# A Mamba scan on one core: program order on the compute engines, softplus sums on GpSimd, diagonals of B through DRAM

## The chip, the core and the metric

The kernel runs on one core of a Trainium2 chip. The core has five engines that run side by side, each through its own queue of instructions: TensorE (PE, matrix products into PSUM; PEld in a profile is its weight load), VectorE (DVE), ScalarE (ACT), GpSimd (POOL[...]) and SyncE (SP), which here issues the DMA transfers. An engine takes its own queue in order; between engines, semaphores make one wait for another. The metric is the device time of one execution in microseconds (us); a run is repeated and the median taken.

## What is computed

Four layers in a row on 8 images of 256 channels and 32 x 32 points, all in fp32: a stack of four Mamba blocks with a channel gate and a batch norm, then three attention layers. Only the Mamba part is touched. For one block, with tokens `xs` (8, 1024, 256):

```python
xn = (xs - mu) * rsqrt(var + 1e-05) * lw + lb
xin, z = split(xn @ iw.T, 2)                    # 512 channels each
xin = silu(causal_conv4(xin) + cb)              # depthwise, 4 taps
proj = xin @ xw.T                               # 16 + 16 + 16 columns
dt = softplus(proj[..., :16] @ dw.T + db)       # (8, 1024, 512)
Bm, Cm = proj[..., 16:32], proj[..., 32:]
A = -exp(alog)                                  # (512, 16)
def step(h, t):                                 # h: (8, 512, 16)
    h = h * exp(dt_t[..., None] * A) + (dt_t * x_t)[..., None] * b_t[:, None, :]
    return h, einsum('bdn,bn->bd', h, c_t)
y = scan(step) + xin * dp
xs = xs + (y * silu(z)) @ ow.T
```

## The kernel before

The Mamba phase works in units: one layer, one image, one half of 512 tokens; 4 x 8 x 2 = 64 units. A unit has 16 steps: 2 pairs of channel tiles (`q`) by 8 groups (`g`) of 2 of the 16 states. In each step TensorE makes the forced term `bx` = B times dt times x by a product with diagonal matrices `dg`; ScalarE makes the decays `da` = exp(dt A); VectorE runs four scans over 512 tokens; GpSimd multiplies the states by C (`ct`, loaded by DMA into all partitions); TensorE sums over the states into `y`, two steps later (LAG = 2).

```python
def forced(s, q, g, i):
    bx = ps_b.tile([P, T, NG], F32, ...)                 # PSUM, 2 buffers
    for k in range(NB):
        for h in range(2):
            for r in range(2):
                nc.tensor.matmul(bx[...], lhsT=s["dtxT"][q][...], rhs=s["dg"][g][h * H:(h + 1) * H, k, :, :], start=True, stop=True)
    return bx

def state(i, k, bx):                                     # cut: the carry of the first half
    for j in range(NG):
        init = 0.0 if c == 0 else st["h"][:, q, g, k, j:j + 1]
        nc.vector.tensor_tensor_scan(hs[i][:, k, j, :], das[i][2 * k + j], bx[:, :, j], init, ALU.mult, ALU.add)

def product(i):
    if s["c"] < NCH - 1:
        nc.scalar.copy(s["st"]["h"][:, q, g, :, :], h[:, :, :, T - 1])      # hc
    nc.gpsimd.tensor_tensor(h, h, cts.pop(i).unsqueeze(1).to_broadcast([P, 2, NG, T]), ALU.mult)
```

The rest of a unit is written as three generators, of which a few pieces are run behind each step: `inward` (norm, input projection, convolution) two units ahead, `onward` (projections to dt, B and C, softplus, the transposed `dtxT`) one unit ahead, `outward` (output projection, residual sum) for the unit before. Each `yield` ends a piece; `AT` says behind which steps the pieces stand.

```python
LAG, AHEAD = 2, 2
AT = ((inward, 2, (0, 1, 2, 3, 5, 6, 8, 9, 11, 12, 13, 14)), (onward, 1, (1, 3, 5, 7, 8, 9, 10, 11, 12)),
      (outward, -1, (3, 4, 6, 7, 9, 10, 11, 12, 13)))
DIAGONALS = (4, 5, 6, 10, 11, 12, 13, 14)
for i in range(len(steps) + LAG):
    n, at = divmod(i, per_unit)
    if i < len(steps):
        ahead(i + AHEAD)                     # load of ct and the 4 decays of step i + 2; 8 buffers da
        bxs = [forced(*steps[i], k) for k in range(2)]
        for k in range(2):
            state(i, k, bxs[k])
        product(i)
    if i >= LAG:
        for j in range(NG):
            summed(s, q, g, j, hs[i - LAG])  # y; dd first where g == 0
        if g == NGR - 1:
            gate(s, q)
    ...                                      # the pieces of AT, then
    if at in DIAGONALS and n + 1 < len(units):
        diagonal(units[n + 1])
```

The pieces that the change and the prediction touch. All PSUM tiles with the tag "mm" share two buffers:

```python
# inward, second piece
rstd = sq[:, 0, :]
nc.scalar.activation(rstd, pvar, AF.Ln, bias=eps)
nc.scalar.activation(rstd, rstd, AF.Exp, scale=-0.5)
nc.vector.tensor_tensor(xn, xn, rstd.unsqueeze(1).to_broadcast([P, CT, T]), ALU.mult)         # L136
# inward, last piece: the gate activation, then the table of exp and ln again
for q in range(DT // 2):
    nc.scalar.activation(s["xin"][q], s["xin"][q], AF.Silu)
nc.scalar.activation(sz, sz, AF.Silu)
exp_ln_table()

# onward
for q in range(DT // 2):
    for r in range(2):
        pd = ps_m.tile([P, T], F32, ..., tag="mm")
        nc.tensor.matmul(pd, lhsT=w["dt"][...], rhs=tokens(proj[...]), start=True, stop=True)
        nc.scalar.activation(e[:, r, :], pd, AF.Abs, bias=col(V_DB + i))
        nc.scalar.activation(dt[:, r, :], pd, AF.Relu, bias=col(V_DB + i))
    nc.scalar.activation(e, e, AF.Exp, scale=-1.0)
    yield
    nc.scalar.activation(one, e, AF.Identity, bias=1.0)
    nc.scalar.activation(ln, one, AF.Ln)
    nc.vector.scalar_tensor_tensor(e, one, 1.0, e, ALU.subtract, ALU.subtract)                # L233
    nc.vector.tensor_tensor(dt, dt, e, ALU.subtract)                                          # L234
    nc.vector.tensor_tensor(dt, dt, ln, ALU.add)                                              # L235
    yield
for q in range(DT // 2):
    for i in range(2):
        nc.gpsimd.tensor_tensor(tokens(dtx[:, i, :]), halves(s["dt"][q][:, i, :]), halves(xin[q][:, i, :]), ALU.mult)
    yield
    for i in range(2):
        pt = ps_m.tile([P, NB, P], F32, ..., tag="mm")
        for k in range(NB):
            nc.tensor.transpose(pt[:, k, :], dtx[:, i, k * P:(k + 1) * P], ident)
        nc.scalar.copy(dtxT[:, i, :, :], pt)
    yield

def diagonal(s):                             # 11 buffers
    nc.gpsimd.tensor_tensor(dg, twin.unsqueeze(1).unsqueeze(3).to_broadcast([P, NB, H, NG]),
                            bt[:, :, NG * g:NG * (g + 1)].unsqueeze(2).to_broadcast([P, NB, H, NG]), ALU.mult)

# outward
for m in range(CT):
    po = ps_m.tile([P, T], F32, ..., tag="mm")
    for i in range(DT):
        nc.tensor.matmul(po, lhsT=w["out"][...], rhs=s["sz"][:, i, :], start=(i == 0), stop=(i == DT - 1))
        if i == 1:
            yield                            # po stays open over a step
    nc.vector.tensor_tensor(x[:, m, :], po, x[:, m, :], ALU.add)                              # xo
```

The instructions are written to a scheduler that keeps their dependences and picks, engine by engine, the order in which they go into the queues. It may pull an instruction ahead of an earlier one that it takes to be waiting. Only the table loads of ScalarE are pinned to their place (`tc.keep_in_program_order`).

Of the kernel before, what the change touches and what calls it, by code (L numbers as in the profile page):

```python
# [19 lines left out]
P = 128  # L20
B, C, HW = 8, 256, 1024
CT = C // P
T = 512
# [13 lines left out]
G_SEB2, G_BNW, G_BNB, G_BQ1, G_BK1, G_BO1, G_BQ2, G_BK2, G_BQ3, G_BK3, G_BO3, G_N = range(0, 24, 2)  # L37


def mamba_phase(tc, ctx, a, spill, ident, gvec, stats):  # L40
    nc = tc.nc
    cst = ctx.enter_context(tc.tile_pool(name="m_cst", bufs=1))
    wp = ctx.enter_context(tc.tile_pool(name="m_w", bufs=1))
    wk1 = ctx.enter_context(tc.tile_pool(name="m_wk1", bufs=1))
# [3 lines left out]
    dgp = ctx.enter_context(tc.tile_pool(name="m_dg", bufs=NGR + 3))  # L48
    dap = ctx.enter_context(tc.tile_pool(name="m_da", bufs=8))
    drp = ctx.enter_context(tc.tile_pool(name="m_dr", bufs=3, space=DRAM))  # L50
    ps_b = ctx.enter_context(tc.tile_pool(name="m_psb", bufs=2, space=PSUM))
    ps_y = ctx.enter_context(tc.tile_pool(name="m_psy", bufs=1, space=PSUM))
    ps_m = ctx.enter_context(tc.tile_pool(name="m_psm", bufs=2, space=PSUM))
# [6 lines left out]
    twin = cst.tile([P, H], F32, name="twin")  # L60
    for r in range(2):
        nc.vector.tensor_copy(twin[r * H:(r + 1) * H, :], ident[r * H:(r + 1) * H, r * H:(r + 1) * H])
    se1 = cst.tile([P, CT, 64], F32, name="se1")
    nc.sync.dma_start(se1, a["se_w1"])
    se2 = cst.tile([64, C], F32, name="se2")
# [39 lines left out]
        nc.sync.dma_start(w["out"], a["m_out"][l])  # L105

    def exp_ln_table():
        tc.keep_in_program_order(nc.scalar.preload_act_table_set("natural_log_exp_and_others"))

    def tokens(t):  # L110

# [5 lines left out]
    def inward(s):  # L117

        l, u, b, c, st = s["l"], s["name"], s["b"], s["c"], s["st"]
        w = s["w"] = layers[l]  # L120
        x = load_x(s, "x")
        pmu = ps_m.tile([P, T], F32, name=f"pmu{u}", tag="mm")
        for k in range(CT):
            nc.tensor.matmul(pmu, lhsT=mean_w, rhs=x[:, k, :], start=(k == 0), stop=(k == CT - 1))
        xn = wk1.tile([P, CT, T], F32, name=f"xn{u}", tag="xn")
        nc.vector.tensor_tensor(xn, x, pmu.unsqueeze(1).to_broadcast([P, CT, T]), ALU.subtract)
        sq = wk1.tile([P, CT, T], F32, name=f"sq{u}", tag="sq")
        nc.scalar.activation(sq, xn, AF.Square)
        yield
        pvar = ps_m.tile([P, T], F32, name=f"pvar{u}", tag="mm")  # L130
        for k in range(CT):
            nc.tensor.matmul(pvar, lhsT=mean_w, rhs=sq[:, k, :], start=(k == 0), stop=(k == CT - 1))
        rstd = sq[:, 0, :]
        nc.scalar.activation(rstd, pvar, AF.Ln, bias=eps)
        nc.scalar.activation(rstd, rstd, AF.Exp, scale=-0.5)
        nc.vector.tensor_tensor(xn, xn, rstd.unsqueeze(1).to_broadcast([P, CT, T]), ALU.mult)  # L136
        yield

        def in_proj(e):
            ps = ps_m.tile([P, T], F32, name=f"pin{u}_{e}", tag="mm")  # L140
            for k in range(CT):
                nc.tensor.matmul(ps, lhsT=w["in"][:, k, e * P:(e + 1) * P], rhs=xn[:, k, :],  # L142
                                 start=(k == 0), stop=(k == CT - 1))
            return ps


        if c == 0:
            st["tail"] = [wk2.tile([P, 2, K - 1], F32, name=f"tail{u}_{q}", tag=f"tail{q}") for q in range(DT // 2)]
        s["xin"] = []
        for q in range(DT // 2):  # L150
            xr = wk1.tile([P, 2, K - 1 + T], F32, name=f"xr{u}_{q}", tag="xr")
            if c == 0:
                nc.gpsimd.memset(xr[:, :, 0:K - 1], 0.0)
            else:
                nc.gpsimd.tensor_copy(xr[:, :, 0:K - 1], st["tail"][q])
            for e in range(2):
                j = 2 * q + e
                ps = in_proj(j)
                nc.scalar.activation(xr[:, e, K - 1:], ps, AF.Identity, bias=w["ib"][:, j:j + 1])
                yield  # L160
            pcs = [ps_m.tile([P, T], F32, name=f"pc{u}_{q}_{r}", tag="mm") for r in range(2)]
            for k in range(K):
                for r in range(2):
                    for e in range(2):
                        j = 2 * q + e
                        nc.tensor.matmul(pcs[r][e * H:(e + 1) * H, :], lhsT=w["cd"][r * H:(r + 1) * H, j * K + k, :],  # L166
                                         rhs=xr[r * H:(r + 1) * H, e, k:k + T], start=(k == 0), stop=(k == K - 1))
            xin = wk5.tile([P, 2, T], F32, name=f"xin{u}_{q}", tag="xin")
            for r in range(2):
                nc.scalar.activation(xin[:, r, :], pcs[r], AF.Identity, bias=w["vec"][:, V_CB + 2 * q + r:V_CB + 2 * q + r + 1])  # L170
            s["xin"].append(xin)
            if c == 0:
                nc.gpsimd.tensor_copy(st["tail"][q], xr[:, :, T:T + K - 1])
            yield

        sz = s["sz"] = wk3.tile([P, DT, T], F32, name=f"sz{u}", tag="sz")
        for e in range(DT):
            ps = in_proj(DT + e)
            nc.scalar.activation(sz[:, e, :], ps, AF.Identity, bias=w["ib"][:, DT + e:DT + e + 1])
            if e < DT - 1:  # L180
# [5 lines that stand above are left out]
        if s["last"] and l + 1 < NL:  # L186
            more_weights(l + 1)
        yield

    def onward(s):  # L190
# [19 lines left out]
            nc.tensor.transpose(pb[:, k, :], proj[X_B:X_B + DS, k * P:(k + 1) * P], ident[X_B:X_B + DS, X_B:X_B + DS])  # L210
        bt = s["bt"] = wk2.tile([P, NB, DS], F32, name=f"bt{u}", tag="bt")
        nc.scalar.copy(bt, pb)
        s["dt"], s["dtxT"], s["dg"] = [], [], []

        for q in range(DT // 2):
            dt = wk3.tile([P, 2, T], F32, name=f"dt{u}_{q}", tag="dt")
            s["dt"].append(dt)
            e = wk1.tile([P, 2, T], F32, name=f"e{u}_{q}", tag="e")
            for r in range(2):
                i = 2 * q + r  # L220
                pd = ps_m.tile([P, T], F32, name=f"pd{u}_{i}", tag="mm")
                nc.tensor.matmul(pd, lhsT=w["dt"][r * H:r * H + DTR, i * P:(i + 1) * P], rhs=tokens(proj[r * H:r * H + DTR, :]),
                                 start=True, stop=True)
# [4 lines that stand above are left out]
            one = wk1.tile([P, 2, T], F32, name=f"one{u}_{q}", tag="dtx")  # L228
            nc.scalar.activation(one, e, AF.Identity, bias=1.0)
            ln = wk1.tile([P, 2, T], F32, name=f"ln{u}_{q}", tag="sq")  # L230
            nc.scalar.activation(ln, one, AF.Ln)  # L231

            nc.vector.scalar_tensor_tensor(e, one, 1.0, e, ALU.subtract, ALU.subtract)  # L233
            nc.vector.tensor_tensor(dt, dt, e, ALU.subtract)  # L234
            nc.vector.tensor_tensor(dt, dt, ln, ALU.add)  # L235
            yield

        for q in range(DT // 2):
# [10 lines left out]
                nc.scalar.copy(dtxT[:, i, :, :], pt)  # L249
            yield  # L250

    def diagonal(s):

        g, bt = len(s["dg"]), s["bt"]
        dg = dgp.tile([P, NB, H, NG], F32, name=f"dg{s['name']}_{g}", tag="dg")
        nc.gpsimd.tensor_tensor(dg, twin.unsqueeze(1).unsqueeze(3).to_broadcast([P, NB, H, NG]),  # L256
                                bt[:, :, NG * g:NG * (g + 1)].unsqueeze(2).to_broadcast([P, NB, H, NG]), ALU.mult)
        s["dg"].append(dg)

    def load_x(s, what):  # L260
# [6 lines left out]
    def outward(s):  # L267
# [36 lines left out]
        exp_ln_table()  # L304
        yield
        for h in range(NCH):
            y = x if h == c else wk1.tile([P, CT, T], F32, name=f"sx{b}_{h}", tag="dtx")
            if h != c:
                nc.sync.dma_start(y, spill[b][h])
            r = wk1.tile([P, CT, T], F32, name=f"res{b}_{h}", tag="e")  # L310
            nc.sync.dma_start(r, a["x"][b].rearrange("(k p) t -> p k t", p=P)[:, :, h * T:(h + 1) * T])
            for m in range(CT):
                nc.vector.scalar_tensor_tensor(y[:, m, :], y[:, m, :], g2[:, m:m + 1], r[:, m, :], ALU.mult, ALU.add)
                nc.vector.bn_stats(stats[:, m, (b * NCH + h) * 6:(b * NCH + h + 1) * 6], y[:, m, :])
            nc.sync.dma_start(spill[b][h], y)
            yield
# [41 lines left out]
    for l in range(NL):  # L358
        for b in range(B):
            st = {}  # L360
            for c in range(NCH):
                units.append({"l": l, "b": b, "c": c, "st": st, "name": f"{l}_{b}_{c}", "last": (b, c) == (B - 1, NCH - 1)})
    steps = [(s, q, g) for s in units for q in range(DT // 2) for g in range(NGR)]
    per_unit = len(steps) // len(units)
    das, cts, hs = {}, {}, {}
# [666 lines left out]
```

## Time and profile before

| | |
|---|---|
| time, median of 3 runs | 10693.12 us (10679.93 to 10694.59) |
| span of the profiled execution | 10677.8 us |
| last scan of the Mamba phase starts at | 8003.1 us |
| TensorE clock granted, mean | 0.961 |
| DMA | 704.91 MB, mean 66 GB/s |

The profile gives, by engine, the busy time and its share of the span; then the span in 40 equal slices, where each digit is the busy share in tenths; then groups of instructions: line of the source, engine, operation, output and inputs by name, shape and count, and behind the bar the busy time and the mean ns of one, and behind the second bar the idle time of the engine just before them with what ended it. The waits list says which engine waited at which line for which line, in total. The timeline lists instructions by start and length. The share of a busy engine is no proof that it is the bound in every stretch: a wait counts only where it is on the path.

### The profile page before, as it was taken

Reading aid. Unit: us, or ns where it says so; the run is one execution under the profiler, and the core shown is the slowest. Engines: PE = TensorE matmul, PEld = TensorE weight load, DVE = VectorE, ACT = ScalarE, POOL = GpSimd, SP = SyncE. Lnnn points to the kernel's source line nnn. Section 1 sums busy time; section 2 is a strip of 40 time slices with the busy share of each in tenths; the row PEclk is TensorE's granted clock in tenths of the full one; section 3 lists DMA queues with packets and bytes.
Section 4 is the critical chain, followed back from the end, with each engine's and each line's share of the span. In section 5 each row is a group of like instructions: output and inputs, shape, how many; then the busy total and the mean of one; then the engine's idle time right before and its main releaser. Section 6 shows DMA issues by size and latency. Waiting matters only on the chain. (4 is left out here: it accounts for less than half of the span.)

```text
span 10677.8 us, 237971 instructions
## 1 busy us (share of the span) xinstructions
PE 9676.4 (91%) x104946; PEld 4868.8 (46%) x104946; DVE 7570.7 (71%) x6419; ACT 6108.2 (57%) x8477; POOL 6709.4 (63%) x2563
## 2 busy tenths in 40 slices
PE   7999998999999989999998988888888999999998
PEld 3444444444444444444444444444443433444433
DVE  4878877777878877877887777777785455544554
ACT  5666666666666766666666666666652233333333
POOL 5777776677777767777776766666671344344346
PEclk9999999999999999999999999999999999999999
DMA  1222222222222222222222222222221000000000
GB/s 64 81 86 86 89 81 81 81 86 84 88 83 82 87 82 86 87 83 84 84 85 83 89 86 86 86 88 88 89 100 40 5 9 9 7 6 1 5 5 9
DMA packets 212557, 704.91 MB, mean 66 GB/s; under 512 B 32640, under 2 KB 33728, under 8 KB 210880
## 3 DMA queue, kind: packets, MB, share of 16 engines
q1 hardware_dynamic: 211520, 689.61, 19.4%
q8 instruction: 830, 13.60, 0.5%
q14 instruction: 207, 1.70, 0.1%
HBM read 637.09 MB, written 52.43 MB: 65 GB/s over the span
## 5 line engine op out<-in xcount | busy, mean ns | idle before, releaser
L392 POOL TENSOR_TENSOR h<-h,ct 128x2048 f32<-128x2048 f32 x1024 | 4683.9, 4581 | 2007.1 <-ACT hc L391 921.9
L335 ACT ACTIVATE da<-dt,A 128x512 f32<-128x512 f32 x4096 | 2847.4, 718 | 2298.7 <-DVE h L385 2283.8
L385 DVE TENSOR_TENSOR_SCAN h<-da,hc,bx 128x512 f32<-128x512 f32 x2048 | 2456.9, 1258 | 692.7 <-PE bx L325 579.9
L385 DVE TENSOR_TENSOR_SCAN h<-da,bx 128x512 f32<-128x512 f32 x2048 | 2332.0, 1198 | 722.9 <-PE bx L325 658.9
L325 PE MATMUL bx<-dg,dtxT 64*64 64x128 f32 x65536 | 2316.7, 281 | 306.1 <-DVE h L385 293.9
L325 PEld LDWEIGHTS bx<-dg,dtxT 64*64 64x64 f32 x65536 | 1950.1, 137 | 1131.0 <-issue 933.4
L349 PE MATMUL y<-h,twin 64*64 64x512 f32 x16384 | 2048.5, 599 | 72.2 <-POOL h L392 72.2
L571 ACT ACTIVATE fp<-fs 128x1024 f32<-128x1024 f32 x768 | 765.4, 1022 | 1435.7 <-PE fs L566 1408.0
L142 PE MATMUL pin<-xn,win 128*128 128x512 f32 x2048 | 1015.9, 619 | 9.8 <-DVE xn L136 5.8
L349 PEld LDWEIGHTS y<-h,twin 64*64 64x64 f32 x16384 | 718.0, 135 | 668.9 <-issue 511.4
L166 PE MATMUL pc<-xr,cd 64*64 64x512 f32 x4096 | 654.1, 695 | 207.8 <-DVE xo L278 207.8
L566 PE MATMUL fs<-fq,fk 32*128 32x512 f32 (+1 forms) x3072 | 723.4, 649 | 56.2 <-ACT fp L652 39.3
L588 DVE TENSOR_TENSOR fz<-fz,fp 128x1024 f32<-128x1024 f32 x384 | 531.3, 1384 | 331.0 <-ACT fp L571 327.0
L588 POOL TENSOR_TENSOR fz<-fz,fp 128x1024 f32<-128x1024 f32 x192 | 477.6, 2487 | 416.2 <-ACT fp L571 412.4
L142 PEld LDWEIGHTS pin<-xn,win 128*128 128x128 f32 x2048 | 349.0, 190 | 676.0 <-issue 405.6
L274 PE MATMUL po<-sz,wo 128*128 128x512 f32 x1024 | 561.7, 676 | 52.3 <-ACT dt L225 52.3
L582 PE MATMUL fo<-fp,fv 128*32 128x512 f32 (+1 forms) x3072 | 597.2, 615 | 0.0
L241 POOL TENSOR_TENSOR dtx<-dt,xin 128x512 f32<-128x512 f32 x256 | 432.8, 1716 | 224.8 <-ACT ln L231 222.2
L256 POOL TENSOR_TENSOR dg<-twin,bt 128x512 f32<-128x512 f32 x512 | 539.0, 1064 | 50.8 <-PE bx L325 37.9
L166 PEld LDWEIGHTS pc<-xr,cd 64*64 64x64 f32 x4096 | 230.4, 154 | 597.2 <-issue 274.5
L235 DVE TENSOR_TENSOR dt<-dt,ln 128x1024 f32<-128x1024 f32 x128 | 470.4, 3675 | 14.4 <-ACT da L335 0.9
L566 PEld LDWEIGHTS fs<-fq,fk 32*128 32x128 f32 (+1 forms) x3072 | 196.1, 185 | 469.4 <-issue 270.2
(391 smaller groups left out, 9160.8 us busy)
## 6 DMA issues: line engine op xcount, KB each, us to landing
ct<-cdr SPq DMA_DIRECT2D x1024, 512.0 KB, 3.7
spill<-xo SPq DMA_DIRECT2D x72, 512.0 KB, 5.3
x<-spill SPq DMA_DIRECT2D x48, 512.0 KB, 4.9
xo<-spill SPq DMA_DIRECT2D x48, 512.0 KB, 3.5
x<-in_x SPq DMA_DIRECT2D x16, 512.0 KB, 5.0
xo<-in_x SPq DMA_DIRECT2D x16, 512.0 KB, 3.7
res<-in_x SPq DMA_DIRECT2D x16, 512.0 KB, 4.2
fx<-spill SPq DMA_DIRECT2D x16, 512.0 KB, 6.4
```

Of the source, the lines that this page charges most:

```text
L142: nc.tensor.matmul(ps, lhsT=w["in"][:, k, e * P:(e + 1) * P], rhs=xn[:, k, :], start=(k == 0), stop=(k == CT - 1))
L166: nc.tensor.matmul(pcs[r][e * H:(e + 1) * H, :], lhsT=w["cd"][r * H:(r + 1) * H, j * K + k, :], rhs=xr[r * H:(r + 1) * H, e, k:k + T], sta ...
L274: nc.tensor.matmul(po, lhsT=w["out"][:, i, m * P:(m + 1) * P], rhs=s["sz"][:, i, :], start=(i == 0), stop=(i == DT - 1))
L325: nc.tensor.matmul(bx[r * H:(r + 1) * H, t:t + H, :], lhsT=s["dtxT"][q][h * H:(h + 1) * H, i, k, r * H:(r + 1) * H], rhs=s["dg"][g][h * H: ...
L335: nc.scalar.activation(da, s["dt"][q][:, i, :], AF.Exp, scale=s["w"]["A"][:, nn:nn + 1])
L349: nc.tensor.matmul(s["y"][r][i * H:(i + 1) * H, :], lhsT=twin[r * H:(r + 1) * H, :], rhs=h[r * H:(r + 1) * H, i, j, :], start=False, stop= ...
L385: nc.vector.tensor_tensor_scan(hs[i][:, k, j, :], das[i][2 * k + j], bx[:, :, j], init, ALU.mult, ALU.add)
L392: nc.gpsimd.tensor_tensor(h, h, cts.pop(i).unsqueeze(1).to_broadcast([P, 2, NG, T]), ALU.mult)
L566: nc.tensor.matmul(scs[h // 2][:, h % 2, :], lhsT=k[r:r + D, m, kt * P:(kt + 1) * P], rhs=q[r:r + D, m, half * T:(half + 1) * T], start=Tr ...
L571: nc.scalar.activation(p, scs[j], AF.Exp, scale=scale)
L582: nc.tensor.matmul(acc["o"][r:r + D, :], lhsT=v[:, kt, m * P + r:m * P + r + D], rhs=ps[h // 2][:, h % 2, :], start=(kt == 0), stop=(kt == ...
L588: add(acc["z"][j], acc["z"][j] if kt > 1 else probs[i - 1][j], ps[j], ALU.add)
```

## The change

Four things, all in the Mamba phase:

- every instruction of TensorE, VectorE, ScalarE and GpSimd is pinned behind the one before it in the source, so that these four queues hold the order of the program. SyncE, and so the DMA issues, stays free;
- the three sums of softplus leave VectorE for GpSimd, with one more pass on ScalarE (1 - one), and the factor of the norm stays in PSUM, so that the product with it reads one operand from SBUF and one from PSUM;
- the diagonals of B are no longer made on GpSimd. Two buffers in DRAM are filled with zeros once; each unit writes its 16 x 512 values of B to their places on the diagonals, in 8 transfers of 512 pieces of 8 bytes, and each diagonal is then loaded whole (256 KB);
- a spare tile at the end of the last layer takes its buffer from another pool.

The aim is that no VectorE instruction of the steady part reads two operands from SBUF while GpSimd works, and that GpSimd has room for the sums.

```diff
--- before.py
+++ after.py
@@ -37,8 +37,28 @@
 G_SEB2, G_BNW, G_BNB, G_BQ1, G_BK1, G_BO1, G_BQ2, G_BK2, G_BQ3, G_BK3, G_BO3, G_N = range(0, 24, 2)
 
 
+class InOrder:
+
+
+    def __init__(self, tc, engine):
+        self.tc, self.engine = tc, engine
+
+    def __getattr__(self, name):
+        def call(*args, **kwargs):
+            return self.tc.keep_in_program_order(getattr(self.engine, name)(*args, **kwargs))
+
+        return call
+
+
+class Engines:
+    def __init__(self, tc):
+        nc = tc.nc
+        self.tensor, self.vector, self.scalar, self.gpsimd = (InOrder(tc, e) for e in (nc.tensor, nc.vector, nc.scalar, nc.gpsimd))
+        self.sync = nc.sync
+
+
 def mamba_phase(tc, ctx, a, spill, ident, gvec, stats):
-    nc = tc.nc
+    nc = Engines(tc)
     cst = ctx.enter_context(tc.tile_pool(name="m_cst", bufs=1))
     wp = ctx.enter_context(tc.tile_pool(name="m_w", bufs=1))
     wk1 = ctx.enter_context(tc.tile_pool(name="m_wk1", bufs=1))
@@ -48,6 +68,7 @@
     dgp = ctx.enter_context(tc.tile_pool(name="m_dg", bufs=NGR + 3))
     dap = ctx.enter_context(tc.tile_pool(name="m_da", bufs=8))
     drp = ctx.enter_context(tc.tile_pool(name="m_dr", bufs=3, space=DRAM))
+    dr1 = ctx.enter_context(tc.tile_pool(name="m_dr1", bufs=1, space=DRAM))
     ps_b = ctx.enter_context(tc.tile_pool(name="m_psb", bufs=2, space=PSUM))
     ps_y = ctx.enter_context(tc.tile_pool(name="m_psy", bufs=1, space=PSUM))
     ps_m = ctx.enter_context(tc.tile_pool(name="m_psm", bufs=2, space=PSUM))
@@ -60,6 +81,13 @@
     twin = cst.tile([P, H], F32, name="twin")
     for r in range(2):
         nc.vector.tensor_copy(twin[r * H:(r + 1) * H, :], ident[r * H:(r + 1) * H, r * H:(r + 1) * H])
+    HALF = H * NB * H * NG
+    diagonals = [dr1.tile([(NGR + 1) * 2 * HALF], F32, name=f"diagonals{k}") for k in range(2)]
+    zero = cst.tile([P, 2 * HALF // P], F32, name="zero")
+    nc.gpsimd.memset(zero, 0.0)
+    for d in diagonals:
+        for g in range(NGR + 1):
+            nc.sync.dma_start(d[g * 2 * HALF:(g + 1) * 2 * HALF].rearrange("(p r) -> p r", p=P), zero)
     se1 = cst.tile([P, CT, 64], F32, name="se1")
     nc.sync.dma_start(se1, a["se_w1"])
     se2 = cst.tile([64, C], F32, name="se2")
@@ -105,7 +133,7 @@
         nc.sync.dma_start(w["out"], a["m_out"][l])
 
     def exp_ln_table():
-        tc.keep_in_program_order(nc.scalar.preload_act_table_set("natural_log_exp_and_others"))
+        nc.scalar.preload_act_table_set("natural_log_exp_and_others")
 
     def tokens(t):
 
@@ -130,10 +158,9 @@
         pvar = ps_m.tile([P, T], F32, name=f"pvar{u}", tag="mm")
         for k in range(CT):
             nc.tensor.matmul(pvar, lhsT=mean_w, rhs=sq[:, k, :], start=(k == 0), stop=(k == CT - 1))
-        rstd = sq[:, 0, :]
-        nc.scalar.activation(rstd, pvar, AF.Ln, bias=eps)
-        nc.scalar.activation(rstd, rstd, AF.Exp, scale=-0.5)
-        nc.vector.tensor_tensor(xn, xn, rstd.unsqueeze(1).to_broadcast([P, CT, T]), ALU.mult)
+        nc.scalar.activation(pvar, pvar, AF.Ln, bias=eps)
+        nc.scalar.activation(pvar, pvar, AF.Exp, scale=-0.5)
+        nc.vector.tensor_tensor(xn, xn, pvar.unsqueeze(1).to_broadcast([P, CT, T]), ALU.mult)
         yield
 
         def in_proj(e):
@@ -210,6 +237,7 @@
             nc.tensor.transpose(pb[:, k, :], proj[X_B:X_B + DS, k * P:(k + 1) * P], ident[X_B:X_B + DS, X_B:X_B + DS])
         bt = s["bt"] = wk2.tile([P, NB, DS], F32, name=f"bt{u}", tag="bt")
         nc.scalar.copy(bt, pb)
+        scatter(s)
         s["dt"], s["dtxT"], s["dg"] = [], [], []
 
         for q in range(DT // 2):
@@ -230,9 +258,10 @@
             ln = wk1.tile([P, 2, T], F32, name=f"ln{u}_{q}", tag="sq")
             nc.scalar.activation(ln, one, AF.Ln)
 
-            nc.vector.scalar_tensor_tensor(e, one, 1.0, e, ALU.subtract, ALU.subtract)
-            nc.vector.tensor_tensor(dt, dt, e, ALU.subtract)
-            nc.vector.tensor_tensor(dt, dt, ln, ALU.add)
+            nc.scalar.activation(one, one, AF.Identity, scale=-1.0, bias=1.0)
+            for t in (one, ln):
+                nc.gpsimd.tensor_tensor(e, e, t, ALU.add)
+            nc.gpsimd.tensor_tensor(dt, dt, e, ALU.add)
             yield
 
         for q in range(DT // 2):
@@ -249,12 +278,21 @@
                 nc.scalar.copy(dtxT[:, i, :, :], pt)
             yield
 
+    def scatter(s):
+
+        d = s["dgd"] = diagonals[s["n"] % len(diagonals)]
+        for h in range(2):
+            for k in range(NB):
+                at = h * HALF + k * H * NG
+                to = d[at:at + NGR * 2 * HALF].rearrange("(g r) -> g r", g=NGR)[:, :H * (NB * H * NG + NG)]
+                to = to.rearrange("g (p r) -> p g r", p=H)[:, :, :NG]
+                nc.sync.dma_start(to, s["bt"][h * H:(h + 1) * H, k, :].rearrange("p (g j) -> p g j", j=NG))
+
     def diagonal(s):
 
-        g, bt = len(s["dg"]), s["bt"]
+        g = len(s["dg"])
         dg = dgp.tile([P, NB, H, NG], F32, name=f"dg{s['name']}_{g}", tag="dg")
-        nc.gpsimd.tensor_tensor(dg, twin.unsqueeze(1).unsqueeze(3).to_broadcast([P, NB, H, NG]),
-                                bt[:, :, NG * g:NG * (g + 1)].unsqueeze(2).to_broadcast([P, NB, H, NG]), ALU.mult)
+        nc.sync.dma_start(dg, s["dgd"][g * 2 * HALF:(g + 1) * 2 * HALF].rearrange("(p b t j) -> p b t j", p=P, b=NB, t=H))
         s["dg"].append(dg)
 
     def load_x(s, what):
@@ -304,7 +342,7 @@
         exp_ln_table()
         yield
         for h in range(NCH):
-            y = x if h == c else wk1.tile([P, CT, T], F32, name=f"sx{b}_{h}", tag="dtx")
+            y = x if h == c else wk2.tile([P, CT, T], F32, name=f"sx{b}_{h}", tag="x")
             if h != c:
                 nc.sync.dma_start(y, spill[b][h])
             r = wk1.tile([P, CT, T], F32, name=f"res{b}_{h}", tag="e")
@@ -359,7 +397,7 @@
         for b in range(B):
             st = {}
             for c in range(NCH):
-                units.append({"l": l, "b": b, "c": c, "st": st, "name": f"{l}_{b}_{c}", "last": (b, c) == (B - 1, NCH - 1)})
+                units.append({"l": l, "b": b, "c": c, "st": st, "n": len(units), "name": f"{l}_{b}_{c}", "last": (b, c) == (B - 1, NCH - 1)})
     steps = [(s, q, g) for s in units for q in range(DT // 2) for g in range(NGR)]
     per_unit = len(steps) // len(units)
     das, cts, hs = {}, {}, {}
```

## The prediction

> **What bounds the kernel now.** I read the page first: busy time by engine, and the 40 slices of the span.
>
> ```profile
> PE 9676.4 (91%) x104946; PEld 4868.8 (46%) x104946; DVE 7570.7 (71%) x6419; ACT 6108.2 (57%) x8477; POOL 6709.4 (63%) x2563
> PE   7999998999999989999998988888888999999998
> DVE  4878877777878877877887777777785455544554
> POOL 5777776677777767777776766666671344344346
> ```
>
> The first 30 slices (about 8030 us) are the Mamba phase, which alone is changed; the attention behind it (about 2650 us) is not, and I carry it over. PE is the fullest engine, at 9 tenths, so what can be won are PE's gaps. They come from the list of waits of 4000 to 5000 us, narrowed to PE (columns: waiter, what it waited for, us in total, times, longest):
>
> ```profile
> PE pc L166 <- DVE xo L278: 27.3, 8, 3.4
> PE bx L325 <- DVE h L385: 25.5, 34, 3.1
> PE pd L222 <- ACT dt L225: 10.4, 8, 1.4
> PE y L349 <- POOL h L392: 7.7, 13, 1.3
> PE pt L248 <- ACT sz L179: 7.6, 9, 1.1
> ```
>
> The first two rows are VectorE being late. Why it is late stands in the groups by line of the same stretch:
>
> ```profile
> L392 POOL TENSOR_TENSOR h<-h,ct 128x2048 f32<-128x2048 f32 x134 | 612.5, 4579 | 231.9 <-ACT hc L391 81.9 <-DVE h L385 64.9 <-PE bx L325 48.5
> L235 DVE TENSOR_TENSOR dt<-dt,ln 128x1024 f32<-128x1024 f32 x16 | 59.5, 3721 | 2.0 <-ACT da L335 0.5
> L233 DVE SCALAR_TENSOR_TENSOR e<-one,e 128x1024 f32<-128x1024 f32 x16 | 19.5, 1216 | 0.0
> L136 DVE TENSOR_TENSOR xn<-xn,sq 128x1024 f32<-128x1024 f32 x8 | 36.5, 4564 | 8.5 <-ACT sq L135 8.5
> ```
>
> L235 and L233 have one size, yet take 3721 and 1216 ns; L136 takes 4564, the length of one GpSimd product (4579). They stand behind that product.
>
> Last the timeline. First, PE where nothing holds it (start, length):
>
> ```profile
> 4141.93 1.90 PE L349 MATMUL y<-h,twin 64*64 64x512 f32 x16
> 4143.75 1.98 PE L142 MATMUL pin<-xn,win 128*128 128x512 f32 x4
> 4145.67 1.98 PE L325 MATMUL bx<-dg,dtxT 64*64 64x128 f32 x64
> 4147.46 1.90 PE L349 MATMUL y<-h,twin 64*64 64x512 f32 x16
> ```
>
> From start to start: y 1.82, pin 1.92, bx 1.79 us. So 3.6 us of PE per step, plus side work. Second, one unit (16 steps), from gate to gate:
>
> ```profile
> 4042.41 1.26 DVE L355 TENSOR_TENSOR sz<-y,sz 128x512 f32<-128x512 f32 x2
> 4162.28 1.26 DVE L355 TENSOR_TENSOR sz<-y,sz 128x512 f32<-128x512 f32 x2
> ```
>
> That is 119.9 us. The side work by the same timeline: pmu, pvar, 8 pin and 4 po halves at 1.92 each, pp 3.5, two pc of 3.75, pt 2.2, pd 2.3, dd 1.7, pb 0.35, together 44.2; with 16 x 3.6 it makes 101.8 us. So PE loses 18 us per unit, 64 units in all.
>
> [...] the trace has 1217 ns at L126, whose second operand is in PSUM. [...] the trace has 4579, and for 1024 elements a median of 2400 (L588), which I use. [...] No transfer of 8 B pieces is in this trace, so their price stays open.
>
> **The change, part by part.**
> 1. Softplus sums and rstd. VectorE loses L233 to L235, (158 + 174 + 470)/64 = 12.5 us per unit, and L136 falls from 4.43 to about 1.22: 15.8 us of its roughly 98. GpSimd gets 6 sums of 2.4 = 14.4 us and loses 8 diagonals, 539/64 = 8.4. ScalarE gets two passes of 1.06 us.
> 2. Diagonals. Per unit 8 scatters of 512 pieces of 8 B, and 8 loads of 256 KB, 2 MB beside the 8 MB of ct. They are made at steps 3 to 14 of the unit before, 11 buffers for 8, so a latency of some us costs nothing. What could cost is the one SyncE queue: ct stands behind the scatter. 4096 pieces over 16 engines are 256 each; at 157 ns (the average packet: 19.4% of 16 x 10678 us over 211520) 40 us, at a third of that 13. The next ct has about 25 us of slack, because GpSimd is then in its sums.
> 3. Program order. Table loads fall from 66 in 1000 us (7.9 per unit) to 2: 7.6 us of ScalarE, which is not the bound. In exchange nothing is pulled ahead any more. I walked one unit by hand: each engine takes its instructions in the order of the source, each starts when its operands and buffer are there. The scans of a step end 5.8 us after its first bx starts (1.27, then 4 x 1.14); the next decays end 0.8 later, since they reuse the scanned buffers; side work of ScalarE comes after them.
>  - Step 3: pin, pb, pd0, pd1, po share two PSUM buffers. pd0 waits for the eviction of pin, behind the decays, and po for Relu of pd0: +3.0 us.
>  - Step 7: one buffer is held by the open po. pd1 waits for Abs and Relu of pd0, which wait for scans and decays (5.8 + 0.8 + 0.2, then 1.3); then pd1 1.05 and po: +4.5 us. Before, po was pulled ahead of pd1 here.
>  - Step 10: pt needs dtx. From the start of step 8: scans 5.8, hc 1.0, product 4.55, sums 7.2, product of step 9 4.55, dtx 1.3 = 24.4. PE gets there after 5.5 + 7.4 + 4.5 = 17.4: +7.0, and +0.7 for the second half.
>  - Step 12, the second dtx behind two products: +2.4. Steps 15 and 0, VectorE the bound: +1.3. y of step 15, whose product waits behind Silu on ScalarE, in every other unit 3.3: +1.6.
>
>  The steps of the unit then start at 0, 5.5, 14.6, 21, 33, 38, 46, 53, 65, 70, 77, 90, 96, 105, 111 and 116 us, and the next unit at 119.4 plus the last 2.9.
>  Sum 20.5, so 101.8 + 20.5 = 122.3 us against 119.9: 2.4 x 64 = 155 us more. The waits on xo and on scans (27.3 + 25.5 in 1000 us, 6.3 per unit) are nearly gone in this walk; the new ones more than eat it up.
> 4. Start. The zeros (18 x 256 KB), scatter and reload, and the inward part of unit 1 that now all stands ahead of the first step: 50 us, an estimate from the first 90 us of the timeline, in which these parts overlapped.
> 5. What a hand walk leaves out, semaphores and ct behind the scatter: 1 us per unit, 64 us.
> 10693 + 155 + 50 + 64 = 10960 us.
>
> **The rivals.**
> (a) VectorE was the cause, and its 15.8 us come back: PE's gaps fall by the 6.3 us above and perhaps as much again by fewer stalls of ScalarE. 64 x 8 = 500 us less, about 10200. For it: the two largest waits of PE. Against: PSUM buffers and GpSimd's sums lie in line with PE, and order can no longer yield.
> (b) The scatter is slow: at 157 ns and more per piece ct lands late, GpSimd stands still and y with it, once per unit, 10 us or more: 11600. For it: 262144 pieces in all against 212557 packets now. Against: the slack of 25 us.
> (c) It cancels: the walk is wrong in its largest stall, because the sums are done earlier (4 us less per unit): about 10700.
>
> **Range and chances.** The walk is good to some 4 us per unit, 256 us either way; the scatter makes the upper side longer. 10650 to 11400. Two per cent are 10479 and 10907. Faster needs stalls under 15 us a unit, where three alone make 15: 0.12. Within 2%: 0.30. Slower: 0.58.
>
> **What would show it.** Right: waits of PE pt on POOL dtx of 5 to 8 us per unit, of PE pd and po on ACT of 5 to 8, no wait of pc on xo; L136 at 1.2 us; table loads near 2 per unit; GpSimd busier by 6 us per unit. Wrong: bx waiting for VectorE as before, ct landing far above its 3.7 us with GpSimd waiting for DMA (rival b), or a unit below 118 us (rival a).

## The result, and the profile after

The changed kernel takes 11118.45 us (median; 11114.17 to 11123.67) against 10686.53: 1.0411 times, 95% interval 1.0386 to 1.0436. It is slower by 432 us. The time lies inside the predicted range of 10650 to 11400 and 158 us above the forecast of 10960.

The page of the changed kernel, busy time by engine, then TensorE and its granted clock in 40 slices:

```profile
PE 9732.8 (88%) x104946; PEld 4831.6 (43%) x104946; DVE 6625.7 (60%) x6035; ACT 5773.4 (52%) x8233; POOL 6938.8 (62%) x2436
PE   6888888888888888888888888888877999999998
PEclk8999999899999989999999898999989999999999
```

VectorE has 945 us less to do, ScalarE 335 less, GpSimd 229 more. None of it is where the time is: TensorE does the same products and is busy 86% of the Mamba phase, where it was 89%. Its mean granted clock (the clock that the chip let it run at, as a share of full speed) fell from 0.961 to 0.926. The scans mark the length of the phase; by number, shortest/median/longest in ns, and the start of the first and last:

```profile
L48 DVE TENSOR_TENSOR_SCAN h<-da,bx x2048: 1190/1195/1223, 156.5 to 8361.8; 128x512 f32<-128x512 f32 x187
L48 DVE TENSOR_TENSOR_SCAN h<-da,hc,bx x2048: 1249/1256/1282, 271.6 to 8444.8; 128x512 f32<-128x512 f32 x187
```

(All pinned instructions carry the line of the helper, L48, so they are told apart by tile.) From first to last scan it is 8288.3 us, before it was 7909.5 (93.6 to 8003.1): 378.8 us over 63.9 units, 5.9 us per unit, 129.6 against 123.7. The first scan starts 62.9 us later. Together 441.7 us; the spans differ by 438.3. What TensorE waits for, 4000 to 5000 us:

```profile
PE pt L48 <- POOL dtx L48: 60.4, 22, 7.4
PE pd L48 <- ACT dt L48: 22.4, 7, 3.3
PE pib L48 <- DMA win<-in_m_in: 12.3, 1, 12.3
PE y L48 <- POOL h L48: 11.7, 4, 2.9
PE pd L48 <- ACT xr L48: 11.2, 8, 1.5
PE po L48 <- ACT dt L48: 9.8, 8, 1.3
PE bx L48 <- DVE h L48: 8.5, 7, 1.3
```

The old first row, pc behind xo with 27.3 us, is gone, and scans hold bx up for 8.5 us, not 25.5. The wait of pib for its weights comes once, where a layer begins. Large now are those that the walk named: pt behind dtx (steps 10 and 12), pd and po behind ScalarE (steps 3 and 7). TensorE around step 10 in the timeline:

```profile
3216.03 1.90 PE L48 MATMUL y<-h,twin 64*64 64x512 f32 x16
3224.85 2.37 PE L48 MATMUL pt<-ident,dtx 128*128 128x128 f32 x8 [6.93 <-POOL dtx L48]
3227.15 3.00 PE L48 MATMUL bx<-dg,dtxT 64*64 64x128 f32 x64
3229.98 1.89 PE L48 MATMUL y<-h,twin 64*64 64x512 f32 x16
```

The gap of 6.93 us is the walk's +7.0. But behind it bx takes 2.83 us from start to start, not 1.79, and pt 2.3, not 1.1. The clock says why; busy time of each engine and granted clock (PEclk, the third number from the end of the line) in four stretches: behind the gaps of steps 10, 3 and 7, and a stretch without a gap:

```profile
3224.80:3230.00 5.20, 5.01 (x76) 4.28 (x80) 0.70 (x1) 1.17 (x2) 5.20 (x2) 0.57 0.44 147
3289.20:3295.40 6.20, 6.14 (x72) 3.61 (x76) 0.60 (x1) 2.10 (x4) 1.32 (x1) 0.60 0.45 90
3321.00:3329.20 8.20, 8.11 (x74) 4.19 (x78) 1.28 (x2) 2.25 (x4) 5.90 (x3) 0.58 0.34 103
3243.70:3256.80 13.10, 12.99 (x192) 6.36 (x185) 11.61 (x11) 8.86 (x12) 9.65 (x3) 1.00 0.24 81
```

In windows of 1 us the clock reads 0.50 at 3228 us and 1.00 at 3230, and the trace has no third level; so the means of 0.57, 0.60 and 0.58 are 4.5, 5.0 and 6.9 us at half clock behind the three gaps. This is in no part of the walk, and it became the third theory (C) of the experiments, beside A (the fixed order makes the waits) and B (the sums on GpSimd or the way through DRAM cost in themselves).

### The profile page after: what moved, and what is told of

It is laid out like the page before. It is cut to its first block, busy times and chain, and to the rows that moved or that the text cites. A ratio compares the mean times of both kernels' runs of the same rounds, so it can differ in the third digit from the quotient of the medians.

```text
span 11116.1 us, 239065 instructions
## 1 busy us (share of the span) xinstructions
PE 9732.8 (88%) x104946; PEld 4831.6 (43%) x104946; DVE 6625.7 (60%) x6035; ACT 5773.4 (52%) x8233; POOL 6938.8 (62%) x2436
## 5 line engine op out<-in xcount | busy, mean ns | idle before, releaser
L48 POOL TENSOR_TENSOR h<-h,ct 128x2048 f32<-128x2048 f32 x1024 | 4640.4, 4536 | 2393.8 <-ACT hc L48 1007.6
L48 ACT ACTIVATE da<-dt,A 128x512 f32<-128x512 f32 x4096 | 2869.0, 720 | 2507.3 <-DVE h L48 2501.9
L48 DVE TENSOR_TENSOR_SCAN h<-da,hc,bx 128x512 f32<-128x512 f32 x2048 | 2453.0, 1261 | 1105.8 <-PE bx L48 1089.9
L48 DVE TENSOR_TENSOR_SCAN h<-da,bx 128x512 f32<-128x512 f32 x2048 | 2329.5, 1201 | 1187.6 <-PE bx L48 1100.7
L48 PEld LDWEIGHTS bx<-dg,dtxT 64*64 64x64 f32 x65536 | 1965.1, 143 | 911.1 <-issue 862.4
L48 PE MATMUL bx<-dg,dtxT 64*64 64x128 f32 x65536 | 2218.2, 287 | 122.5 <-DVE h L48 111.4
L48 PE MATMUL y<-h,twin 64*64 64x512 f32 x16384 | 1991.5, 601 | 95.1 <-POOL h L48 91.1
L48 PE MATMUL pin<-xn,win 128*128 128x512 f32 x2048 | 1016.7, 620 | 11.2 <-DVE xn L48 8.1
L48 PEld LDWEIGHTS y<-h,twin 64*64 64x64 f32 x16384 | 605.9, 137 | 758.0 <-issue 650.3
L48 PE MATMUL po<-sz,wo 128*128 128x512 f32 x1024 | 706.5, 828 | 76.0 <-ACT dt L48 76.0
L48 PE MATMUL pt<-ident,dtx 128*128 128x128 f32 x1024 | 230.7, 365 | 591.1 <-POOL dtx L48 541.2
L48 PEld LDWEIGHTS pin<-xn,win 128*128 128x128 f32 x2048 | 349.1, 190 | 673.5 <-issue 311.1
L48 PE MATMUL pd<-proj,wdt 16*128 16x512 f32 x512 | 267.4, 742 | 289.4 <-ACT dt L48 201.6
L48 PEld LDWEIGHTS pt<-ident,dtx 128*128 128x128 f32 x1024 | 148.3, 181 | 740.4 <-POOL dtx L48 705.9
L48 PE MATMUL pc<-xr,cd 64*64 64x512 f32 x4096 | 466.5, 589 | 0.0
L48 PEld LDWEIGHTS po<-sz,wo 128*128 128x128 f32 x1024 | 236.3, 250 | 487.3 <-issue 352.7
```

The lines of the kernel that those rows point to most:

```text
L48: return self.tc.keep_in_program_order(getattr(self.engine, name)(*args, **kwargs))
```

## The experiments

Each ratio is to the kernel before on the same chip.

**The order left free.** The pinning taken back (table loads stay pinned), all else as changed:

```diff
-            return self.tc.keep_in_program_order(getattr(self.engine, name)(*args, **kwargs))
+            return getattr(self.engine, name)(*args, **kwargs)
```

> The changed kernel with only the pinning taken back (table loads stay pinned): sums still on GpSimd, diagonals still through DRAM. Theory A (the fixed order makes the waits, the sums on GpSimd are harmless if other work may pass them): pt waiting for dtx falls from 60 us in 1000 to under 20, pd and po waiting for ScalarE from 43 to under 20, time 10450 to 10700. Theory B (the sums or the DRAM path themselves cost, whatever the order): 10950 or more. Theory C (half of the loss is TensorE's clock, which falls after a gap): the granted clock goes back from 0.926 to 0.95 or more if, and only if, the gaps go.

10501.45 us, ratio 0.9824 (0.9808 to 0.9841), clock 0.963; pt waits 19.7 us in 1000, pd and po on ScalarE 22.5 together, a little over the 20 expected. So the pinning costs 617 us and the other parts of the change win 185. Theory A holds for the result; theory B falls.

**The order alone.** The kernel before, pinned (with the spare tile's buffer as in the change):

```diff
-    nc = tc.nc
+    nc = Engines(tc)
```

> The kernel before with the pinning alone (and the spare tile's buffer moved, as in the change): sums on VectorE, diagonals on GpSimd. Theory A: the waits of steps 3 and 7 are there (pd and po on ScalarE, some 35 to 45 us in 1000), the wait of pt on dtx is small[...]; 10850 to 11100. Theory B: 10700, as before, because neither the sums on GpSimd nor the DRAM path is there.

11407.34 us, ratio 1.0676 (1.0658 to 1.0694), clock 0.932: more than expected. The largest wait of TensorE is bx behind the scans, 77.9 us in 1000, and one row of VectorE in the groups shows what a fixed queue does with a slow instruction:

```profile
L48 DVE SCALAR_TENSOR_TENSOR e<-one,e 128x1024 f32<-128x1024 f32 x15 | 48.9, 3258 | 44.2 <-ACT one L48 44.2
```

The first sum stands in the queue ahead of the next scans: it waits 2.9 us for ScalarE's `one`, then takes 3.3 us instead of the 1.2 of the kernel before, and no scan may pass it. Pinning costs 720 us here and 617 in the changed kernel.

**The sums back on VectorE, pinned.**

```diff
-            nc.scalar.activation(one, one, AF.Identity, scale=-1.0, bias=1.0)
-            for t in (one, ln):
-                nc.gpsimd.tensor_tensor(e, e, t, ALU.add)
-            nc.gpsimd.tensor_tensor(dt, dt, e, ALU.add)
+            nc.vector.scalar_tensor_tensor(e, one, 1.0, e, ALU.subtract, ALU.subtract)
+            nc.vector.tensor_tensor(dt, dt, e, ALU.subtract)
+            nc.vector.tensor_tensor(dt, dt, ln, ALU.add)
```

> The changed kernel with the three sums of softplus back on VectorE (and without the pass 1 - one): order pinned, diagonals through DRAM, rstd in PSUM. Theory A: the wait of pt on dtx, 60 us in 1000, falls under 15; 7.7 us per unit of gap and some 2 us of slow clock behind it go[...]: 10550 to 10800. Theory B for the DRAM path: still 11000 or more.

11416.71 us, ratio 1.0682 (1.0664 to 1.0700): slower than the changed kernel by 298 us, not faster. This expectation was wrong. The wait of pt did fall, from 60.4 to 20.2, but bx now waits 51.5 us in 1000 for the scans and another 20.7 that the profile puts down to issue; VectorE stands 40.6 us before the first sum. The sums on GpSimd make the largest single wait and are still the better place: on VectorE the scans behind them have to wait. Beside the order alone (11407) the kernel differs by the norm's factor and the way through DRAM, and the time is the same.

**Six and seven products to fill the gap of step 10.** In the changed kernel, overwritten by the transposes that follow:

```diff
+                if q == 0 and i == 0 and s["n"]:
+                    for _ in range(6):
+                        nc.tensor.matmul(pt.rearrange("p k t -> p (k t)"), lhsT=mean_w, rhs=xin[q][:, 0, :], start=True, stop=True)
                 for k in range(NB):
                     nc.tensor.transpose(pt[:, k, :], dtx[:, i, k * P:(k + 1) * P], ident)
```

> The changed kernel with six matrix products more per unit, whose results are overwritten: they stand on TensorE ahead of the first transposes of dtx at step 10, where it otherwise waits some 7 us, and keep it busy for some 6 us. Theory C[...]: the transposes and the bx behind them run at full length again, 2 us less per unit, 10960 to 11020 and a higher granted clock although work is added. If the gap costs only its own length: 11118 or a little more.

11049.53 us, ratio 1.0342 (1.0319 to 1.0365), clock 0.946: 69 us faster than the changed kernel with 378 products (6 in each of 63 units) more to do. Less than expected; the trace shows 1.70 and 0.58 us of the gap still open and bx behind it at 2.72 us from start to start in one unit. So once more, with 7 and 1:

```diff
-                if q == 0 and i == 0 and s["n"]:
-                    for _ in range(6):
+                if q == 0 and s["n"]:
+                    for _ in range(1 if i else 7):
```

> As e5, with seven products ahead of the first transposes and one between the two halves, so that less than 1 us of the gap at step 10 stays open (in e5 1.7 and 0.6 us stayed, and bx behind it still took 2.9 us in the trace). Theory C: bx and pt at step 10 at full length, 2.2 us per unit less than in the changed kernel, 10960 to 11010. If TensorE's clock is set by something else: 11050 to 11120, as e5 or more.

11004.06 us, ratio 1.0317 (1.0300 to 1.0335), clock 0.950. TensorE around step 10 of one unit:

```profile
4080.58 6.28 PE L48 MATMUL pt<-xin,mean_w 128*128 128x512 f32 x14
4088.05 0.66 PE L48 MATMUL pt<-ident,dtx 128*128 128x128 f32 x4 [1.19 <-POOL dtx L48]
4088.54 1.02 PE L48 MATMUL pt<-xin,mean_w 128*128 128x512 f32 x2
4089.40 0.60 PE L48 MATMUL pt<-ident,dtx 128*128 128x128 f32 x4
4089.93 1.98 PE L48 MATMUL bx<-dg,dtxT 64*64 64x128 f32 x64
4091.73 1.90 PE L48 MATMUL y<-h,twin 64*64 64x512 f32 x16
```

bx takes 1.80 us from start to start again. By the ratios (1.0317 against 1.0411) useless work makes the kernel about 100 us faster, 1.6 us per unit where 2.2 were expected. Theory C holds at step 10: the gap costs its own length and the slow stretch behind it.

**The diagonals on GpSimd again, pinned.**

```diff
-        nc.sync.dma_start(dg, s["dgd"][g * 2 * HALF:(g + 1) * 2 * HALF].rearrange("(p b t j) -> p b t j", p=P, b=NB, t=H))
+        nc.gpsimd.tensor_tensor(dg, twin.unsqueeze(1)...to_broadcast([P, NB, H, NG]), bt[...]...to_broadcast([P, NB, H, NG]), ALU.mult)
```

> The changed kernel with the diagonals made on GpSimd again (no zeros, no scatter, no loads): order pinned, sums on GpSimd. If the DRAM path costs (rival b of the prediction): faster than 11118, 11000 or less. If it is hidden and what counts is GpSimd's room: 8 x 1.06 us per unit come back onto GpSimd, where pt and y already wait for it at steps 8 to 12, so up to 8 us per unit more: 11200 to 11600.

11111.64 us, ratio 1.0405 (1.0388 to 1.0423), against 1.0411 for the changed kernel: no difference. Neither expectation was right. The waits are the same row by row (pt 61.3, pd 22.4 and 11.1, y 11.6). The way through DRAM is fully hidden, and GpSimd's room that it makes is not used either: the 8.4 us of diagonals fit into GpSimd's own waits.

**What the free order gains by.** The free kernel with the sums back on VectorE; the norm's factor in PSUM and the diagonals through DRAM stay. Either the sums on VectorE or the other two parts make the 185 us. The edit is that of the sums above, on the kernel with free order.

> The changed kernel with the order free and the sums of softplus on VectorE: what is left of the change are the factor of the norm in PSUM and the diagonals through DRAM. It splits the 185 us that the change without its order wins. [...] near the kernel before, 10600 to 10690. If the norm's product (4.4 to 1.2 us) or GpSimd's freed time brought it: 10450 to 10550.

10688.11 us, ratio 1.0016 (1.0006 to 1.0026): within 0.3% of the kernel before. Its waits are back too, by the list of TensorE's waits:

```profile
PE pc L48 <- DVE xo L48: 27.3, 8, 3.4
PE bx L48 <- DVE h L48: 24.0, 28, 2.2
```

So the 185 us come with the move of the sums. The norm's product at 1.22 us instead of 4.43 and the way through DRAM bring nothing together. Whether the sums would win as much without those two was not tried in a free order.

**The two waits for PSUM buffers undone, pinned.** The output product runs in one piece, the first pd a step later:

```diff
-                if i == 1:
-                    yield
@@ onward, behind the copy of B and its scatter
+        yield
@@
-(onward, 1, (1, 3, 5, 7, 8, 9, 10, 11, 12)), (outward, -1, (3, 4, 6, 7, 9, 10, 11, 12, 13))
+(outward, -1, (3, 6, 9, 10, 11, 12, 13)), (onward, 1, (1, 3, 4, 5, 7, 8, 9, 10, 11, 12))
```

> The changed kernel with the side work placed so that no product waits for a PSUM buffer at steps 3 and 7: po runs in one piece at steps 3 and 6, pb stays at 3, the first pd goes to 4. Order still pinned, same instructions in number. Theory A with the clock: the waits of pd and po on ScalarE (43 us in 1000, 5.4 per unit) and the slow stretches behind them (some 6 us per unit) go: 10400 to 10650. Without the clock term, only 5.4 us per unit: 10750 to 10850. If the order as such costs, through something else: over 10950.

10441.13 us, ratio 0.9774 (0.9758 to 0.9790), clock 0.952: 677 us less than the changed kernel, 10.6 per unit. The waits of pd and po (43.4 us in 1000 by 7.72 units, 5.6 per unit) cannot pay for that alone; with the slow stretches behind them (6.0 by the timeline) it is 11.6. In 1000 us without the start of a layer TensorE is busy 893.73 us at a mean clock of 0.95 (4000 to 5000 us), in the changed kernel 863.20 at 0.91 (3000 to 4000). Of units of 119.1 us (scans from 155.8 to 7769.2) and of 129.6 that is 106.4 and 111.9: 5.5 us less for the same products, and 5.1 less idle time. The wait of pt is left, 68.2.

**Rebalanced, pinned.** As the last, and the second half of softplus, of dtx and of pt is moved into the unit that uses it, and the sums are spread. The new places, with the pieces listed as comments:

```diff
+(onward, 1, (1, 3, 4, 5, 6, 7, 9, 10, 11, 12)), (onward_late, 0, (1, 2, 4, 6, 7))
+# onward:      pp | pb, scatter | pd 0 | one, ln, sum | sum | sum | dtx 0 | pd 1 | pt 0 | pt 0
+# onward_late: one, ln, 2 sums | sum | dtx 1 | pt 1 | pt 1
+# outward at (4, 7, ...); one has a buffer of its own, which res of the last layer shares
```

> As e6, and the second half of softplus (its sums, dtx and pt) moved to steps 1 to 7 of the unit that uses it, the sums one or two to a step, so that GpSimd never has more than 5 us besides its product. Same instructions in number, order pinned. Theory A: no wait of TensorE above 1 us is left but at steps 15 and 0; a unit near 106 us, 9800 to 10100, granted clock 0.97 or more. If pinning as such is worse than the scheduler's choice: above 10500.

9624.20 us, ratio 0.9013 (0.8998 to 0.9028), clock 0.983. The same instructions in number on every compute engine as the changed kernel, the same pinning, 1494 us less, and below the range that was expected. All that TensorE waits for from 4000 to 5000 us:

```profile
PE y L48 <- POOL h L48: 14.5, 5, 2.9
PE bx L48 <- DVE h L48: 11.0, 9, 1.3
```

And one unit, from the bx of step 5 to the next:

```profile
4304.34 1.98 PE L48 MATMUL bx<-dg,dtxT 64*64 64x128 f32 x64
...
4407.20 1.98 PE L48 MATMUL bx<-dg,dtxT 64*64 64x128 f32 x64
```

102.9 us, where the sum of TensorE's work in the prediction was 101.8. The mean unit from first to last scan is 106.6.

**Rebalanced, free.** The same with the scheduler's order; the edit is that of the first experiment.

> As e8, but the order left to the scheduler. Theory A (order in itself is neither good nor bad, waits are): within 1.5% of e8, 9800 to 10200. If the scheduler's choice was what mattered in the first place: faster than e8 by over 2%.

9797.73 us, ratio 0.9175 (0.9159 to 0.9192), 1.8% slower than pinned. Here y waits 30.4 us in 1000 for GpSimd, 22 times, against 14.5 and 5. A little outside the 1.5% expected: order is not neutral, and here a good one written down is better than the scheduler's.

**Rebalanced, diagonals on GpSimd.** The edit is that of the diagonals above.

> The rebalanced pinned kernel (9624) with the diagonals made on GpSimd instead of through DRAM. There GpSimd is 88% busy in the steady part, so 8.5 us more per unit of some 105 no longer fit without reaching y: 9750 to 10100. If GpSimd still finds the room, as it did in the changed kernel (11112 against 11118): within 0.5% of 9624.

9618.16 us, ratio 0.9020 (0.9004 to 0.9035): the same as through DRAM. Busy time in the stretch (PE, PEld, DVE, ACT, POOL, then clock, DMA share, GB/s), first with DRAM, then with GpSimd:

```profile
4000.00:5000.00 1000.00, 970.35 (x13808) 512.86 (x13800) 770.50 (x686) 720.60 (x1085) 875.96 (x278) 0.99 0.39 119
```

```profile
4000.00:5000.00 1000.00, 960.77 (x13706) 507.98 (x13704) 763.53 (x680) 718.72 (x1075) 950.61 (x367) 0.99 0.30 99
```

GpSimd is busy 95% of this stretch, and the time does not change.

**Rebalanced, sums on VectorE.** Pinned; the three sums as in the kernel before, one or two to a step. Either they hold up the scans here too, or they cost only where VectorE is late anyway.

> The rebalanced pinned kernel (9624) with the sums of softplus on VectorE. Theory A: [...] a sum of 1.2 us takes up to 4.6 and the scans and bx wait: 6 sums by some 1 to 2 us of TensorE per unit, 9900 to 10300. [...] within 1% of 9624.

10210.05 us, ratio 0.9575 (0.9559 to 0.9591): 586 us more than on GpSimd, 9 per unit. By the groups of 4000 to 5000 us the first and last sum take 2218 and 2576 ns on average, the middle one 1211, and VectorE stands 45.4 us before the first; bx waits 52.2 us for scans. So the last purpose of the change stands: moving the sums off VectorE is worth 185 us in a free order, 298 in the changed one (11417 against 11118), 586 in a balanced one.

## Why the prediction was right, and where not

**The verdict and its mechanism.** The walk of the queues held: the waits that it named (pt; pd and po) make 103.8 of the 137.1 us of TensorE's waits in the list after, and both sums, 7.8 and 5.6 us per unit, lie in the 5 to 8 that were given as signs. Slower had a chance of 0.58. Of the other signs, the norm's product takes 1.22 us and table loads are 2.1 per unit, as said; GpSimd is busier by 3.6 us per unit, not 6, since dtx (1716 to 1294 ns) and the product (4581 to 4536 ns) became shorter.

**The sizes of the waits.** With 7.72 units in 1000 us the rows give, per unit: pt 7.8 (the walk: 7.7 + 2.4 for steps 10 and 12), pd and po 5.6 (3.0 + 4.5, of which 1.0 is work that now runs one after the other), y 1.5 (1.6), bx 1.1 (1.3). Each was a little too large, step 12 most: 1.4 us in the unit above.

**The term that was missing: TensorE's clock.** The step that failed is "the sum 101.8 + 20.5": it counted every product at the length that it has where nothing holds it. By the timeline the products behind the three gaps take longer by 2.2 us (step 10), 2.7 (step 3) and 3.3 (step 7), 8.2 in one unit. The granted clock says about the same: 5.2 us at a mean of 0.57 lose 2.2, 6.2 at 0.60 lose 2.5, 8.2 at 0.58 lose 3.4. TensorE from first to last scan (its busy time is the first number behind the comma), before and after:

```profile
93.60:8003.10 7909.50, 7073.24 (x92862) 3767.97 (x92854) 6207.06 (x5069) 5228.60 (x7522) 5639.31 (x2022) 0.96 0.26 85
156.50:8444.80 8288.30, 7104.97 (x92748) 3720.73 (x92748) 5267.48 (x4690) 4878.74 (x7264) 5869.41 (x1899) 0.91 0.31 98
```

It is idle 13.1 us per unit before and 18.5 after. So the unit after is 101.8 of work, 18.5 idle and 9.3 by which the products are longer: 129.6. The walk's 20.5 was 2.0 too large, its products 9.3 us too short. That the total missed by so little is in part luck: the unit of 119.9 us that stood for the kernel before is 3.8 shorter than its mean unit (123.7), and 1 us per unit had been added for semaphores. 9.3 - 2.0 - 1 - 3.8 makes the 2.5 us between the rise of 3.4 that was forecast (2.4 and 1) and the 5.9 measured, 160 us in 64 units.

The slow clock is no novelty of the change either. In the unit measured before it was 0.87 over 13.0 us and 0.82 over 9.3 us, 1.7 us lost each. I took the 119.9 as measured and did not split these off, so the walk set waits alone against waits and slow products. In the totals, 5.4 of the 5.9 us are idle time, and the busy time is almost the same; of the 8.8 us per unit by which the busy time before stands above 101.8, the two stretches explain 3.4, and the rest stays open. The page showed the clock in its second part, and I did not read it.

Two smaller slips: the items of the side work add up to 44.4, not 44.2; and with its own 50 us of start and 1 us per unit, faster would have needed stalls under 13 us a unit, not 15.

**The start.** 50 us forecast, 62.9 measured.

**Rival (a), VectorE's time comes back.** Wrong as the outcome, right as a part: with a free order its two largest waits (pc for xo, bx for scans) go from 52.8 to 9.8 us in 1000 and 185 us are won, not 500. The removal of L233 to L235 from VectorE wins; of the 4.43 us of the norm nothing came back where the sums stayed on VectorE.

**Rival (b), the scatter.** Wrong. 512 pieces of 8 B land in a median of 4.7 us, a loaded diagonal in 4.0, and ct in 3.7, as before. Two kernels with and without DRAM differ by less than their intervals, pinned and rebalanced. GpSimd's 6 us per unit more, which I put into the sum of its work, decided nothing either; what counted was its place: 7.2 us of sums came in one piece ahead of a product and dtx, and with the pieces spread the wait of pt is gone from the list.

**Rival (c), it cancels.** It did not: the largest stall was 6.93 us in the unit above and 7.4 at most from 4000 to 5000 us, where the walk had 7.0.

**Where theory A failed.** I expected that the sums back on VectorE would take the wait of step 10 away and gain 300 to 550 us. The wait went and the kernel lost 298. The walk had been done for one of the two places only.

**What stays open.** Whether the 3.3 us that y of step 15 was forecast to wait is all Silu on ScalarE was not tried apart; its row stays at 11 to 15 us in 1000 in all pinned kernels. Nor was each of the waits at steps 3 and 7 undone by itself, nor each of the four queues pinned by itself, nor the norm's factor taken back where the sums are on GpSimd.

## What to carry to other kernels

A queue in fixed order is only as good as the places of its pieces: walk one period by hand, for every engine and every shared buffer, before pinning, and move the pieces until the engine that bounds the time hardly waits. In this kernel a fixed order was then better than the scheduler's (9624 against 9798 us); before, it was worse (11118 against 10501). A gap on TensorE can cost more than its length (6.93 us at step 10, and 2.2 us of longer products behind it): read the granted clock behind it, in the kernel before as well, and count the slow products. And an engine's free time is no gain where its work already fits between its waits: the diagonals taken off GpSimd were worth nothing (11118 us through DRAM against 11112, 9624 against 9618), nor was the shorter product of the norm (1.22 us, not 4.43) where it was tried.

## What the hardware showed that was not expected

The clock falls at gaps that I would have taken for harmless. The trace has it at two levels, 0.50 and 1.00. At step 10 it fell inside the gap of 6.93 us (0.73 from 3222 to 3223 us, then 0.50). At step 7 it fell just behind one of 3.14 us (0.95 from 3321.0 to 3321.5 us, then 0.50). At step 3 it fell in the pd between one of 1.32 and one of 1.22 us (0.82 from 3287.0 to 3287.5 us, then 0.50), with a mean of 0.60 over the 6.2 us from 3289.2 on. Gaps of 0.8 and 0.6 us (step 12) and of 1.3 us (step 15) left the clock at 1.00 (3240 to 3244 and 3255 to 3266 us) and the next bx at 1.80 and 1.79 us. Step 3 after:

```profile
3286.52 1.52 PE L48 MATMUL pd<-proj,wdt 16*128 16x512 f32 x4 [1.32 <-ACT xr L48]
3289.26 3.78 PE L48 MATMUL po<-sz,wo 128*128 128x512 f32 x4 [1.22 <-ACT dt L48]
```

The same po takes 1.92 us from start to start where no gap is near. Step 3 of the kernel before shows it behind a single gap of 0.88 us, with a mean clock of 0.57 over 4062 to 4066 us:

```profile
4061.94 3.18 PE L274 MATMUL po<-sz,wo 128*128 128x512 f32 x4 [0.88 <-ACT dt L225]
```

So the length of one gap does not decide alone: the clock fell at one of 0.88 us and stayed at 1.00 at one of 1.28. What does decide is not shown. At step 3 small products (pb and pd, on 16 partitions) stand beside the gap; whether they bear on the clock was not tried.
